# Output weights of a scan layer: rows and means three steps earlier, half of the centring on VectorE

## The chip, the cores and the metric

One core of one Trainium2 chip runs the whole program. The metric is the device time of one execution in microseconds (us), the median of three runs. TensorE (PE) multiplies matrices, VectorE (DVE), ScalarE (ACT) and GpSimd (POOL) work elementwise, SyncE (SP) and POOL issue DMA transfers. Each engine works off its own instructions in order, and the queue of SP as well: a transfer whose inputs are not ready holds all that stand behind it.

## The reference

Two layers on an image batch x of 2 x 768 x 64 x 64 in f32. Cut to what matters, the first layer is:

```
h   = preact(x)                                    # group norm, statistics over the whole image
xs  = conv3x3_depthwise(h @ in_proj_w.T)           # 1536 channels
u   = xs * sigmoid(xs)
dt, B, C = split(u @ x_proj_w.T)                   # 48 + 4 + 4
delta = softplus(dt @ dt_w + dt_b)
s[l]  = exp(delta * A) * s[l-1] + delta * u * B    # scan over 4096 positions, 4 states
y   = sum_n(s * C) + D * u
y   = (y - mean(y)) * rsqrt(var(y) + 1e-5) * ln_g + ln_b   # over the 1536 channels
x1  = x + y @ out_proj_w.T
```

The second layer normalises x1 and is an attention-like product over channels with two 768 x 768 matrices. The edits lie in the first layer, before its scan starts. The kernel folds the normalisation of y into the output weights: with W the 1536 x 768 matrix out_proj_w.T, it needs W scaled by ln_g row by row, less the mean over the 1536 channels of that scaled matrix (a row of 768 numbers, the same for all channels), and as a bias ln_b @ W. "Centring" is that subtraction.

## The kernel before

The image is cut into 16 tiles of 8 rows (512 positions), the 1536 channels into 12 blocks of 128. A chunk is one block of one tile; there are 192 chunks, numbered n for the input projection, a = n - 2 for the convolution, g = n - 17 for the scan. One call of `step(g)` issues the work of all three, so each is a software pipeline written out by hand: the order of instructions on each engine is the order of the calls, and nothing reorders it.

The first sixteen calls (v = 0 to 15, n = v, a = v - 2) only fill the pipeline. In each, PE does `row0(n)` (L348: the first image row for n below 12), `in_proj(n)` (L362) and what `products_of(v)` adds at the end of the step; ACT does `tap_act` (L415, the centre tap into PSUM, `acc`), what `scalar_of(v)` adds, `in_proj_evict` (L374 to L377), `norm_x` (L317, the input of the next tile; three of them at v = 11, needed by `in_proj(12)`), `taps_act` (L427, two taps into buffers) and `silu` (L468). DVE does the remaining taps (`taps_dve`, L461) and the statistics of the second image (L154). POOL adds the two ACT taps by accumulating DMA: `taps_dma` (L439) of chunk a, which waits for the sum of that chunk's taps, and `taps_dma_sum` (L433) of chunk a + 1. SP loads input weights (L323, 384 KB, four buffers), x (L307; one each at v = 6, 7 and 8, three at v = 11, 256 KB each) and the statistics input (L149).

The output weights go along: four loads of three 128 x 768 blocks each (L246, `wg`, at v = 2 to 5), their rows of ln_g @ W and ln_b @ W by PE at v = 11 (`out_weights_rows`, L256, into PSUM tag po0, in three groups of 256 columns), a copy of those rows by ACT (L264), the mean spread over 128 partitions and the bias by PE at v = 12 (L272 and L273, into tag pz), its copy to `wmean` (L277 to L279), twelve scalings by ACT (L283) and twelve subtractions, eight on POOL and four on DVE (L287), in steps 13 to 15, and twelve stores by SP to `wo_dr` in DRAM (L290), from which the out-projection later loads (L329). Blocks 0 to 2 are stored after step 14, the other nine after step 15 and behind it.

Then the pool `l0st` (rows, wmean, pick, wg) is released and the pool `late` takes its place on the same side of SBUF: `ysum`, `bc` (B and C broadcast), `s`, the two `da` buffers of the scan and five tap buffers `tm`. `step(-1)` comes next: `x_dbl` (L491) with its store of B and C to `bc_dr` (L492), the first dt product (`dt_pair`, L502, tag pz) with its softplus, `load_bc` (L495) and the exponentials (L514). `step(0)` begins with the first scan on DVE: L537, L539 and L546.

Of the kernel before, what the change touches and what calls it, by code (L numbers as in the profile page):

```python
# [7 lines left out]
F32 = mybir.dt.float32  # L8
AF = mybir.ActivationFunctionType
ALU = mybir.AluOpType  # L10
# [4 lines left out]
P = 128  # L15
NB, DM, H, W = 2, 768, 64, 64
# [3 lines left out]
NS = 4  # L20
RX = R + 2 * NS
KM = DM // P
# [9 lines left out]
TL = TR * W  # L32
# [8 lines left out]
PC_W, PC_A, PC_D, PC_CB, PC_DB, PC_G, PC_B, PC_N = 0, 9, 13, 14, 15, 16, 17, 18  # L41
# [11 lines left out]
AHEAD = 15  # L53
# [14 lines left out]
def both_layers(  # L68
# [10 lines left out]
    pc = wp.tile([P, KI, PC_N], F32, name="pc")  # L79
# [48 lines left out]
    psZ = ctx.enter_context(tc.tile_pool(name="l0_psz", bufs=1, space=PSUM))  # L128
    psX = ctx.enter_context(tc.tile_pool(name="l0_psx", bufs=1, space=PSUM))
    psO = ctx.enter_context(tc.tile_pool(name="l0_pso", bufs=1, space=PSUM))  # L130
# [114 lines left out]
    def out_weights_load(wg, k):  # L245
        nc.sync.dma_start(wg[k // 3], out_wT[k * P : (k + 3) * P, :].rearrange("(k p) m -> p k m", p=P))  # L246

    MG = 2 * P  # L250

    def out_weights_rows(wg):
        gb = psO.tile([P, 512], F32, tag="po0", name="pgb")
        for k in range(KI):
            for j in range(KM // 2):
                nc.tensor.matmul(  # L256
                    gb[32 * j : 32 * j + 2, :MG], pc[:, k, PC_G : PC_B + 1], wg[k // 3][:, k % 3, j * MG : (j + 1) * MG],
                    start=(k == 0), stop=(k == KI - 1),
                )
        return gb  # L260

    def out_weights_rows_copy(gb, rows):
        for j in range(KM // 2):
            nc.scalar.copy(rows[32 * j : 32 * j + 2, :], gb[32 * j : 32 * j + 2, :MG])  # L264

    def out_weights_mean(rows, pick):
        wm = psZ.tile([P, 2, 512], F32, tag="pz", name="pwm")
        pb = wm[:, 1, MG : MG + KM]
        for j in range(KM // 2):
            for e in range(2):  # L270
                m = 2 * j + e
                nc.tensor.matmul(pb[:, m : m + 1], rows[:, e * P : (e + 1) * P], pick[:, j, P : P + 1], start=True, stop=True)  # L272
            nc.tensor.matmul(wm[:, j // 2, j % 2 * MG : (j % 2 + 1) * MG], pick[:, j, :P], rows, start=True, stop=True)  # L273
        return wm, pb

    def out_weights_mean_copy(wm, pb, wmean):
        nc.scalar.copy(wmean[:, : 2 * MG], wm[:, 0, :])  # L277
        nc.scalar.copy(wmean[:, 2 * MG :], wm[:, 1, :MG])
        nc.scalar.copy(bias_o, pb)  # L279

    def out_weights_scale(wg, k):
        w = wg[k // 3][:, k % 3, :]
        nc.scalar.activation(w, w, AF.Copy, scale=pc[:, k, PC_G : PC_G + 1])  # L283

    def out_weights_sub(wg, wmean, k, engine):
        w = wg[k // 3][:, k % 3, :]
        engine.tensor_sub(w, w, wmean)  # L287

    def out_weights_store(wg, k):
        nc.sync.dma_start(  # L290
            wo_dr[:, k // 3, :, k % 3, :].rearrange("q p m -> p q m"), wg[k // 3][:, k % 3, :].rearrange("p (q m) -> p q m", m=2 * P)
        )
# [50 lines left out]
            )  # L343

    def row0(n):
        p0 = psZ.tile([P, 512], F32, tag="pz", name=f"pa0_{n}")
        for k in range(KM):
            nc.tensor.matmul(p0[:, :W], wis[n][:, k, :], x0s[0][:, k, :], start=(k == 0), stop=(k == KM - 1))  # L348
        nc.scalar.copy(carry[n][:, 1, :], p0[:, :W])
        if n == KI - 1:  # L350
            give(x0s.pop("tile"))
# [803 lines left out]
    with tc.manual_schedule():  # L1155
# [31 lines left out]
        def step(g, prep=None, acts=None):  # L1187
# [13 lines left out]
            if n < KI:  # L1201
                row0(n)
# [148 lines left out]
                norms[g + 2][0][0]()  # L1351

        with tc.tile_pool(name="l0st", bufs=1, side="right") as sp:
            rows = sp.tile([P, MG], F32, name="gb_rows")
            nc.vector.memset(rows, 0.0)
            wmean = sp.tile([P, DM], F32, name="wmean")
            pick = sp.tile([P, KM // 2, P + 1], F32, name="pick")
            nc.sync.dma_start(pick, pick_in)
            wg = [sp.tile([P, 3, DM], F32, name=f"wg{q}") for q in range(KI // 3)]

            first = -AHEAD - 2
            scaled_w = {13: ((0, 1), (2,)), 14: ((3, 4, 5), (6,)), 15: ((7, 8, 9), (10, 11))}
            held = {}

            def products_of(v):
                if v == 11:
                    held["rows"] = out_weights_rows(wg)
                if v == 12:
                    held["mean"] = out_weights_mean(rows, pick)

            def scalar_of(v):
                if v == 12:
                    out_weights_rows_copy(held["rows"], rows)
                if v == 13:
                    out_weights_mean_copy(*held["mean"], wmean)
                for k in sum(scaled_w.get(v, ((), ())), ()):
                    out_weights_scale(wg, k)

            for v in range(AHEAD + 1):
                if 2 <= v < 6:  # L1380
                    out_weights_load(wg, 3 * (v - 2))
                step(first + v, lambda: products_of(v), lambda: scalar_of(v))
                if v == 0:
                    nc.scalar.activation(neg_a, pc[:, :, PC_A : PC_A + NS], AF.Exp)
                    nc.scalar.mul(neg_a, neg_a, -1.0)
                for k in scaled_w.get(v, ((), ()))[0]:
                    out_weights_sub(wg, wmean, k, nc.gpsimd)
                for k in scaled_w.get(v - 1, ((), ()))[1]:
                    out_weights_sub(wg, wmean, k, nc.vector)
                for k in sum(scaled_w.get(v - 1, ((), ())), ()):  # L1390
                    out_weights_store(wg, k)
            for k in scaled_w[AHEAD][1]:
                out_weights_sub(wg, wmean, k, nc.vector)
            for k in sum(scaled_w[AHEAD], ()):
                out_weights_store(wg, k)

        late = right.enter_context(tc.tile_pool(name="l0l", bufs=1, side="right"))

        ysum = late.tile([P, 3, TL], F32, name="ysum")
        bc = late.tile([P, 2 * NS, TL], F32, name="bc")  # L1400
        s = late.tile([P, NS, TL + 1], F32, name="s")

        da1 = late.tile([P, NS, TL + 1], F32, name="da1")
        tm_bufs = [late.tile([P, TL], F32, name=f"tm{j}") for j in (0, 3, 1, 2, 4)]
        tm_bufs = [tm_bufs[j] for j in (0, 2, 3, 1, 4)]
        das = [late.tile([P, NS, TL + 1], F32, name="da0"), da1]
        nc.gpsimd.memset(das[0][:, :, 0], 0.0)
        step(-1)
        nc.gpsimd.memset(das[1][:, :, 0], 0.0)
# [70 lines left out]
@with_exitstack  # L1480
def mamba_then_attention(
    ctx, tc, x, in_wP, xp_wP, dt_wP, out_wT, pc_in, comb_in, pick_in, xsum_in, qkvP, woutP, temp_c, ident_in, gavg_in, gsel_in, hcol_in, hsel_in, esel_in, out
):
    nc = tc.nc
    keep = ctx.enter_context(tc.tile_pool(name="keep", bufs=1))
    dram = ctx.enter_context(tc.tile_pool(name="dram", bufs=1, space=DRAM))
    x1 = [dram.tile([DM, L], F32, name=f"x1_{b}") for b in range(NB)]

    stats1 = [keep.tile([P, KM, 2 * NT + 1], F32, name=f"stats1_{b}") for b in range(NB)]

    ident = keep.tile([P, P], F32, name="ident")
    nc.sync.dma_start(ident, ident_in)
    ones = keep.tile([P, P], F32, name="ones")
    nc.vector.memset(ones, 1.0)
    eps_c = keep.tile([P, 1], F32, name="eps_c")
    nc.vector.memset(eps_c, EPS)
    consts = (ident, ones, eps_c)


    wo_dr = dram.tile([KM // 2, KI // 3, P, 3, 2 * P], F32, name="wo_dr")  # L1500
    bc_dr = [dram.tile([2 * NS, TL], F32, name=f"bc_dr{i}") for i in range(NI)]

    s_dr = {k: dram.tile([KM // 2, 4, P, KM // 2, P], F32, name=f"s_dr_{k}") for k in ("p1", "p3")}
    both_layers(
        tc, nc, consts, x, in_wP, xp_wP, dt_wP, out_wT, pc_in, comb_in, pick_in, xsum_in, gavg_in, gsel_in, wo_dr, bc_dr, s_dr, x1, stats1,
        qkvP, woutP, temp_c, hcol_in, hsel_in, esel_in, [out[b].rearrange("c h w -> c (h w)") for b in range(NB)],
    )
# [105 lines left out]
```

## Time and profile before

| what | us |
|---|---|
| median of three runs | 3709.17 |
| the runs | 3709.97, 3709.17, 3702.92 |
| span of the profiled execution (no other time of that execution is given) | 3708.1 |
| PE, DVE, ACT, POOL busy | 3555.3, 2842.1, 2571.8, 1782.8 |
| first scan operation (L537) starts, from the start of the span | 190.81 |

A line of the timeline reads: start, duration, engine, source line, operation, output <- input, number of instructions, and in brackets how long the engine stood idle before it and what ended that. PE and POOL busy times are as the profile has them; DMA-issuing instructions are on POOL and on SP's queue (SPq). In a line of stretches the columns are the stretch, its sum, then busy time of PE, PE's weight loads, DVE, ACT and POOL, the clock that PE was granted as a share of full, the DMA share and GB/s. Transfers land later than their issue; the landing times are those of their packets in the trace.

### The profile page before, as it was taken

To read this page: it belongs to the slowest core of one execution; us is meant where nothing else is said; L and a number is where in the kernel's file an instruction comes from. 1 tells how busy PE (TensorE), PEld (TensorE's weight loads), DVE (VectorE), ACT (ScalarE), POOL (GpSimd) and SP (SyncE) were. 2 spreads that over 40 slices of the span, in tenths; PEclk is the share of its full clock that TensorE was granted. 3 is DMA by queue.
4 is the path that set the end of the run, shared out by engine and by line. 5 is a ranking of instruction groups with operands and counts; after the bars stand their busy time and mean duration, and the time that the engine had idled before them with its cause. 6 is when DMAs were issued, how large, how long until landed. Compare 5 with 4: busy or idle time off the path is not lost. (4 is left out here: it accounts for less than half of the span.)

```text
span 3708.1 us, 37935 instructions
## 1 busy us (share of the span) xinstructions
PE 3555.3 (96%) x11176; PEld 1771.0 (48%) x11176; DVE 2842.1 (77%) x2571; ACT 2571.8 (69%) x5026; POOL 1782.8 (48%) x1813
## 2 busy tenths in 40 slices
PE   5968999999999999999999999999999999999999
PEld 3423333343333333333344333433347658886688
DVE  7899999999999999999999999997721362224522
ACT  2688889888988898888888988897633542244221
POOL 0355565565655655555556655654443313330232
PEclk9978999999999999999999999999999999999999
DMA  9877888998989899898898989997676538763487
GB/s 354 232 169 162 182 204 185 205 211 191 212 176 209 201 200 208 184 204 185 187 203 194 212 175 211 203 201 177 142 202 183 192 93 265 256 205 123 158 268 245
DMA packets 380301, 738.98 MB, mean 199 GB/s; under 512 B 44304, under 2 KB 116944, under 8 KB 376000
## 3 DMA queue, kind: packets, MB, share of 16 engines
q0 software_dynamic: 146208, 270.08, 42.6%
q1 hardware_dynamic: 233888, 466.49, 38.4%
q8 instruction: 90, 1.47, 0.2%
q14 instruction: 115, 0.94, 0.1%
HBM read 440.96 MB, written 60.03 MB: 135 GB/s over the span
## 5 line engine op out<-in xcount | busy, mean ns | idle before, releaser
L362 PE MATMUL pa<-u,w 128*128 128x512 f32 (+1 forms) x2304 | 1035.8, 599 | 7.5 <-ACT carry L377 7.3
L603 PE MATMUL po<-u,w 128*128 128x512 f32 x2256 | 1011.5, 598 | 8.1 <-DVE u L615 7.9
L539 DVE TENSOR_TENSOR_SCAN s<-da,s 128x2052 f32<-128x2052 f32 x192 | 851.1, 4433 | 19.5 <-DVE s L537 0.9
L362 PEld LDWEIGHTS pa<-u,w 128*128 128x128 f32 x2304 | 429.5, 192 | 597.7 <-issue 484.7
L603 PEld LDWEIGHTS po<-u,w 128*128 128x128 f32 x2256 | 420.8, 190 | 582.7 <-issue 551.3
L526 POOL TENSOR_TENSOR ysum<-da 128x1024 f32<-128x1024 f32 x192 | 386.8, 2015 | 547.4 <-DVE da L546 464.1
L461 DVE SCALAR_TENSOR_TENSOR acc<-xs,pc,acc 128x512 f32<-128x512 f32 x698 | 525.6, 753 | 29.2 <-ACT acc L415 12.7
L537 DVE TENSOR_TENSOR s<-du,bc 128x2048 f32<-128x2048 f32 x192 | 439.2, 2288 | 83.0 <-POOL du L518 73.8
L433 POOL DMA_DIRECT2D tm<-tm x309 | 270.3, 875 | 462.7 <-ACT tm L427 423.5
L514 ACT ACTIVATE da<-dl,neg_a 128x512 f32<-128x512 f32 x768 | 489.6, 713 | 0.0
L546 DVE TENSOR_TENSOR da<-s,bc 128x2048 f32<-128x2048 f32 x192 | 440.0, 2292 | 6.3
L533 POOL DMA_DIRECT2D u<-ysum x384 | 380.4, 1255 | 4.2 <-issue 3.5
L427 ACT ACTIVATE tm<-xs,pc 128x512 f32<-128x512 f32 x486 | 317.1, 717 | 15.1 <-DMA tm<-tm 7.3
L415 ACT ACTIVATE acc<-xs,pc 128x512 f32<-128x512 f32 x192 | 132.2, 688 | 215.7 <-DVE u L461 206.4
L518 POOL TENSOR_TENSOR du<-dl,u 128x512 f32<-128x512 f32 x192 | 246.5, 1284 | 0.0
L439 POOL DMA_DIRECT2D u<-tm x177 | 206.1, 1164 | 59.6 <-issue 50.1
L447 PE MATMUL acc<-xs,dg 128*128 128x512 f32 x264 | 140.0, 641 | 50.0 <-ACT acc L415 49.6
L886 PE MATMUL po_p<-v,w 128*128 128x256 f32 x672 | 171.9, 380 | 1.4 <-ACT po_p L983 1.4
L886 PE MATMUL po_p<-u,w 128*128 128x256 f32 x624 | 159.7, 379 | 0.0
L461 DVE SCALAR_TENSOR_TENSOR u<-xs,pc,acc 128x512 f32<-128x512 f32 x192 | 143.6, 748 | 7.7
L831 POOL TENSOR_TENSOR v<-u 128x256 f32<-128x256 f32 x21 | 15.7, 758 | 277.1 <-ACT u L849 262.1
L886 PE MATMUL acc_p<-u,w 128*128 128x256 f32 x556 | 143.7, 382 | 4.6 <-DMA w<-woutP 3.4
(285 smaller groups left out, 5006.5 us busy)
## 6 DMA issues: line engine op xcount, KB each, us to landing
u<-ysum POOLq DMA_DIRECT2D x384, 256.0 KB, 5.5
tm<-tm POOLq DMA_DIRECT2D x309, 256.0 KB, 4.3
w<-in_wP SPq DMA_DIRECT2D x192, 384.0 KB, 4.4
w<-wo_dr SPq DMA_DIRECT2D x192, 384.0 KB, 4.7
u<-x SPq DMA_DIRECT2D x263, 256.0 KB, 4.8
w<-s_dr_p SPq DMA_DIRECT2D x288, 192.0 KB, 3.4
u<-tm POOLq DMA_DIRECT2D x177, 256.0 KB, 5.8
bc<-bc_dr SPq DMA_DIRECT2D x32, 1024.0 KB, 7.7
```

The source lines that it names most:

```text
L362: nc.tensor.matmul(pa[:, :nn], w[:, k, :], xts[i, k][:, :nn], start=(k == 0), stop=(k == KM - 1))
L427: nc.scalar.activation(tm.rearrange("p (h w) -> p h w", w=W), xs[:, dy : dy + TR, dx : dx + W], AF.Copy, scale=pc[:, c, PC_W + j : PC_W + ...
L433: nc.gpsimd.dma_start(tms[a][0], tms[a][q], accum_op=ALU.add)
L461: nc.vector.scalar_tensor_tensor(dst, xs[:, dy : dy + TR, dx : dx + W], pc[:, c, PC_W + j : PC_W + j + 1], acc, ALU.mult, ALU.add)
L514: nc.scalar.activation(das[g % 2][:, n, 1:], deltas[g], AF.Exp, scale=neg_a[:, c, n : n + 1])
L526: nc.gpsimd.tensor_add(ysum[:, 0 : 2 + g % 2 : 1 + g % 2, :], da[:, 0:2, 1:], da[:, 2:4, 1:])
L533: nc.gpsimd.dma_start(us[g], ysums(g, n), accum_op=ALU.add)
L537: nc.vector.tensor_mul(s[:, :, 1:], dus.pop(g).unsqueeze(1).to_broadcast([P, NS, TL]), bc[:, :NS, :])
L539: nc.vector.tensor_tensor_scan(sf, das[g % 2].rearrange("p n l -> p (n l)"), sf, 0.0, ALU.mult, ALU.add)
L546: nc.vector.tensor_mul(das[g % 2][:, :, 1:], s[:, :, 1:], bc[:, NS:, :])
L603: nc.tensor.matmul(po[e], w[:, kk, e * P : (e + 1) * P], us[i * KI + k], start=(k == 0), stop=(k == KI - 1))
L886: nc.tensor.matmul(dst, half[:, k, :], tiles[blocks[seq[i][0]][:3]][what][k], start=(start and k == 0), stop=(k == KH - 1), skip_group_che ...
```

## The change

It does five things. The rows are computed at v = 8 and the mean at v = 9. The rows are formed in four column groups of 192, not three of 256, and the mean by four products of 192 columns with twelve short ones of 64 for the bias. Scales, centring and stores are spread over v = 9 to 15: blocks 0, 2, 4, 6 and 9 are scaled by ACT a step before POOL subtracts the mean (v = 10 to 14), and blocks 1, 3, 5, 7, 8, 10 and 11 are scaled and centred by one DVE scalar_tensor_tensor that reads the mean from PSUM (v = 11 to 15); each step's blocks are stored right after that step. PSUM tags change hands: the rows take pz, `row0` takes po0, the mean stays in pz until the last centring. And the buffers of `late` are allocated in another order, `da0` and three of the `tm` first.

```diff
--- before.py
+++ after.py
@@ -247,44 +247,51 @@
 
 
 
-    MG = 2 * P
+    MJ = DM // 4
+    HP = P // 2
 
     def out_weights_rows(wg):
-        gb = psO.tile([P, 512], F32, tag="po0", name="pgb")
+        gb = psZ.tile([P, 2, 512], F32, tag="pz", name="pgb")[:, 0, :]
         for k in range(KI):
-            for j in range(KM // 2):
+            for j in range(4):
                 nc.tensor.matmul(
-                    gb[32 * j : 32 * j + 2, :MG], pc[:, k, PC_G : PC_B + 1], wg[k // 3][:, k % 3, j * MG : (j + 1) * MG],
+                    gb[32 * j : 32 * j + 2, :MJ], pc[:, k, PC_G : PC_B + 1], wg[k // 3][:, k % 3, j * MJ : (j + 1) * MJ],
                     start=(k == 0), stop=(k == KI - 1),
                 )
         return gb
 
     def out_weights_rows_copy(gb, rows):
-        for j in range(KM // 2):
-            nc.scalar.copy(rows[32 * j : 32 * j + 2, :], gb[32 * j : 32 * j + 2, :MG])
+        for j in range(4):
+            nc.scalar.copy(rows[32 * j : 32 * j + 2, :], gb[32 * j : 32 * j + 2, :MJ])
 
     def out_weights_mean(rows, pick):
         wm = psZ.tile([P, 2, 512], F32, tag="pz", name="pwm")
-        pb = wm[:, 1, MG : MG + KM]
-        for j in range(KM // 2):
-            for e in range(2):
-                m = 2 * j + e
-                nc.tensor.matmul(pb[:, m : m + 1], rows[:, e * P : (e + 1) * P], pick[:, j, P : P + 1], start=True, stop=True)
-            nc.tensor.matmul(wm[:, j // 2, j % 2 * MG : (j % 2 + 1) * MG], pick[:, j, :P], rows, start=True, stop=True)
+        pb = wm[:, 1, 2 * MJ : 2 * MJ + KM]
+        for h in range(2 * KM):
+            m, e = divmod(h, 2)
+            j, o = divmod(h * HP, MJ)
+            nc.tensor.matmul(
+                pb[e * HP : (e + 1) * HP, m : m + 1], rows[:, o : o + HP], pick[:, j, P : P + 1], start=True, stop=True
+            )
+        for j in range(4):
+            nc.tensor.matmul(wm[:, j // 2, j % 2 * MJ : (j % 2 + 1) * MJ], pick[:, j, :P], rows, start=True, stop=True)
         return wm, pb
 
     def out_weights_mean_copy(wm, pb, wmean):
-        nc.scalar.copy(wmean[:, : 2 * MG], wm[:, 0, :])
-        nc.scalar.copy(wmean[:, 2 * MG :], wm[:, 1, :MG])
+        nc.scalar.copy(wmean, wm[:, :, : 2 * MJ])
         nc.scalar.copy(bias_o, pb)
 
     def out_weights_scale(wg, k):
         w = wg[k // 3][:, k % 3, :]
         nc.scalar.activation(w, w, AF.Copy, scale=pc[:, k, PC_G : PC_G + 1])
 
-    def out_weights_sub(wg, wmean, k, engine):
-        w = wg[k // 3][:, k % 3, :]
-        engine.tensor_sub(w, w, wmean)
+    def out_weights_sub(wg, wmean, k):
+        w = wg[k // 3][:, k % 3, :].rearrange("p (h m) -> p h m", h=2)
+        nc.gpsimd.tensor_sub(w, w, wmean)
+
+    def out_weights_centre(wg, wm, k):
+        w = wg[k // 3][:, k % 3, :].rearrange("p (h m) -> p h m", h=2)
+        nc.vector.scalar_tensor_tensor(w, w, pc[:, k, PC_G : PC_G + 1], wm[:, :, : 2 * MJ], ALU.mult, ALU.subtract)
 
     def out_weights_store(wg, k):
         nc.sync.dma_start(
@@ -343,7 +350,7 @@
             )
 
     def row0(n):
-        p0 = psZ.tile([P, 512], F32, tag="pz", name=f"pa0_{n}")
+        p0 = psO.tile([P, 512], F32, tag="po0", name=f"pa0_{n}")
         for k in range(KM):
             nc.tensor.matmul(p0[:, :W], wis[n][:, k, :], x0s[0][:, k, :], start=(k == 0), stop=(k == KM - 1))
         nc.scalar.copy(carry[n][:, 1, :], p0[:, :W])
@@ -1351,29 +1358,31 @@
                 norms[g + 2][0][0]()
 
         with tc.tile_pool(name="l0st", bufs=1, side="right") as sp:
-            rows = sp.tile([P, MG], F32, name="gb_rows")
+            rows = sp.tile([P, MJ], F32, name="gb_rows")
             nc.vector.memset(rows, 0.0)
-            wmean = sp.tile([P, DM], F32, name="wmean")
-            pick = sp.tile([P, KM // 2, P + 1], F32, name="pick")
+            wmean = sp.tile([P, 2, DM // 2], F32, name="wmean")
+            pick = sp.tile([P, 4, P + 1], F32, name="pick")
             nc.sync.dma_start(pick, pick_in)
             wg = [sp.tile([P, 3, DM], F32, name=f"wg{q}") for q in range(KI // 3)]
 
             first = -AHEAD - 2
-            scaled_w = {13: ((0, 1), (2,)), 14: ((3, 4, 5), (6,)), 15: ((7, 8, 9), (10, 11))}
+            centred = {
+                10: ((0,), ()), 11: ((2,), (1,)), 12: ((4,), (3,)), 13: ((6,), (5,)), 14: ((9,), (7, 8)), 15: ((), (10, 11))
+            }
             held = {}
 
             def products_of(v):
-                if v == 11:
+                if v == 8:
                     held["rows"] = out_weights_rows(wg)
-                if v == 12:
+                if v == 9:
                     held["mean"] = out_weights_mean(rows, pick)
 
             def scalar_of(v):
-                if v == 12:
+                if v == 9:
                     out_weights_rows_copy(held["rows"], rows)
-                if v == 13:
+                if v == 10:
                     out_weights_mean_copy(*held["mean"], wmean)
-                for k in sum(scaled_w.get(v, ((), ())), ()):
+                for k in centred.get(v + 1, ((), ()))[0]:
                     out_weights_scale(wg, k)
 
             for v in range(AHEAD + 1):
@@ -1383,27 +1392,23 @@
                 if v == 0:
                     nc.scalar.activation(neg_a, pc[:, :, PC_A : PC_A + NS], AF.Exp)
                     nc.scalar.mul(neg_a, neg_a, -1.0)
-                for k in scaled_w.get(v, ((), ()))[0]:
-                    out_weights_sub(wg, wmean, k, nc.gpsimd)
-                for k in scaled_w.get(v - 1, ((), ()))[1]:
-                    out_weights_sub(wg, wmean, k, nc.vector)
-                for k in sum(scaled_w.get(v - 1, ((), ())), ()):
+                on_pool, on_vector = centred.get(v, ((), ()))
+                for k in on_pool:
+                    out_weights_sub(wg, wmean, k)
+                for k in on_vector:
+                    out_weights_centre(wg, held["mean"][0], k)
+                for k in on_pool + on_vector:
                     out_weights_store(wg, k)
-            for k in scaled_w[AHEAD][1]:
-                out_weights_sub(wg, wmean, k, nc.vector)
-            for k in sum(scaled_w[AHEAD], ()):
-                out_weights_store(wg, k)
 
         late = right.enter_context(tc.tile_pool(name="l0l", bufs=1, side="right"))
 
+        da0 = late.tile([P, NS, TL + 1], F32, name="da0")
+        tm_bufs = {j: late.tile([P, TL], F32, name=f"tm{j}") for j in (1, 2, 4)}
         ysum = late.tile([P, 3, TL], F32, name="ysum")
+        tm_bufs.update({j: late.tile([P, TL], F32, name=f"tm{j}") for j in (0, 3)})
         bc = late.tile([P, 2 * NS, TL], F32, name="bc")
         s = late.tile([P, NS, TL + 1], F32, name="s")
-
-        da1 = late.tile([P, NS, TL + 1], F32, name="da1")
-        tm_bufs = [late.tile([P, TL], F32, name=f"tm{j}") for j in (0, 3, 1, 2, 4)]
-        tm_bufs = [tm_bufs[j] for j in (0, 2, 3, 1, 4)]
-        das = [late.tile([P, NS, TL + 1], F32, name="da0"), da1]
+        das = [da0, late.tile([P, NS, TL + 1], F32, name="da1")]
         nc.gpsimd.memset(das[0][:, :, 0], 0.0)
         step(-1)
         nc.gpsimd.memset(das[1][:, :, 0], 0.0)
@@ -1544,8 +1549,8 @@
     comb[[0, 32], 0, :] = 1.0 / DI
     comb[[64, 96], 1, :] = 1.0 / DI
 
-    pick = np.zeros((P, KM // 2, P + 1), np.float32)
-    for j in range(KM // 2):
+    pick = np.zeros((P, 4, P + 1), np.float32)
+    for j in range(4):
         pick[32 * j, j, :P] = 1.0 / DI
         pick[32 * j + 1, j, P] = 1.0
```

## The prediction

> **What bounds the kernel now.** I read the page first (PE busy 96% of the span, so the layers themselves are PE's), then the 40 slices, whose first one is the only one with PE under 0.8 (5968...). The edits all lie in that start, the sixteen fill steps before the first scan, so I went to the waits between 110 and 200 us:
>
> ```profile
> DVE s L537 <- DMA bc<-bc_dr: 8.3, 1, 8.3
> POOL da L1407 <- DMA wo_dr<-wg: 5.9, 1, 5.9
> ACT tm L427 <- DMA wo_dr<-wg: 5.4, 1, 5.4
> ```
>
> The first scan waits for the broadcast of B and C; the two others wait for the stores of the output weights. The timeline of SP, POOL, DVE and PE (start, duration, engine, line) shows how these meet:
>
> ```profile
> 119.46 1.37 SPq L307 DMA_DIRECT2D u<-x  x3
> ...
> 157.17 2.68 SPq L290 DMA_DIRECT2D wo_dr<-wg  x3
> ...
> 169.79 9.98 SPq L290 DMA_DIRECT2D wo_dr<-wg  x9
> ...
> 183.53 0.81 SPq L495 DMA_DIRECT2D bc<-bc_dr  x2
> ```
> ```profile
> 141.49 0.89 POOL L433 DMA_DIRECT2D u<-u  x1
> ...
> 164.51 5.66 POOL L287 TENSOR_TENSOR wg<-wg,wmean 128x768 f32<-128x768 f32 x3
> ...
> 172.28 5.65 POOL L287 TENSOR_TENSOR wg<-wg,wmean 128x768 f32<-128x768 f32 x3
> ```
> ```profile
> 164.09 8.64 DVE L287 TENSOR_TENSOR wg<-wg,wmean 128x768 f32<-128x768 f32 x3
> ...
> 190.81 2.29 DVE L537 TENSOR_TENSOR s<-du,bc 128x2048 f32<-128x2048 f32 x1 [8.25 <-DMA bc<-bc_dr]
> ```
>
> Read backwards: POOL's last subtraction ends at 177.9, SP issues the last store at 179.13, it lands at 183.48 (4.35 us), and at 183.53 the broadcast starts. Its first half lands at 190.32 and the scan begins 0.49 us later. The broadcast waits for all twelve stores although its buffer reaches over the first group of weights only, by the order of allocation, and that group had landed at 164.78: the wait is for the whole pool. After 190.81 DVE runs some dozen steps without a wait and PE follows, so a shift of the first scan carries to the end one to one. The number to predict is when that scan starts.
>
> **The change, part by part.** *Rows and means three steps sooner.* The PE rows they cost now are:
>
> ```profile
> 133.55 5.36 PE L256 MATMUL pgb<-wg,pc 128*2 128x256 f32 x72
> 138.84 5.42 PE L362 MATMUL pa<-u,w 128*128 128x512 f32 x12
> ```
>
> 72 passes in 5.29 us are 73.5 ns a pass. Four groups make 96 passes of 192 columns. If the pace follows columns and groups (73.5 x 3/4 x 3/4 = 41 ns) that is 4.0 us, if it follows passes 7.1; no row decides it, I take the middle, 5.6. The mean took 2.64 us (144.09 to 146.73). Now it has 24 short passes, between 92 ns (L272's four in 0.37) and half of that, since each loads 64 columns of weights where L272's loads 128, and 8 of 192 columns at 0.19 (L273's two of 256 in 0.51, by columns): 2.6 to 3.7, taken 3.3. So PE carries 8.9 us (6.6 to 10.8) two to four steps sooner; in_proj(10) ends near 135.9 instead of 126.97 and in_proj(11) near 142.4. By itself this costs nothing later, since the same work leaves steps 11 and 12.
>
> A rule speaks against the four groups: the Trainium skill, "TensorE: Matmul & The Clock Gate", section "Wait — 56ns, not 53.3ns?", has the sequencer spend about 62 ns on each MATMUL where hardware decode is off. By it 96 passes take 6.0 us as an estimate, more than the 5.29 measured for 72; no row here shows such a floor for this shape.
>
> *Stores sooner, and what they stand in front of.* Each store now follows its step. In the order of the changed build, SP's queue after step 10 is store 0, the weights of in_proj(13), one statistics load, then the three x loads of tile 1 that in_proj(12) needs. Store 0 waits for POOL's subtraction 0, which stands behind L433 of a=9. That L433 was issued at 141.49 (its ACT input would now be ready near 139 to 141, so nothing brings it sooner). Add its 0.89 and one subtraction (3.91 for two, 2.0): 144.4. Then four SP issues of some 0.42 to 0.46: the x loads go out at 145.6 to 146.5 where they went at 119.46 to 120.41. They landed 5.2 to 6.6 us after issue; the last now lands near 152.4.
>
> Queued behind: ACT's three L317 are in order ahead of the tap copies of a=10, so ACT holds from about 146 to 150.8. in_proj(12) starts near 142.4, finds k=3 to 5 missing, and ends near 154.2 (last norm 153.2, one us of passes): in_proj(13), 146.73 before, is 7.5 us later. The tap copies end at 154.5, ACT's acc(11) at 155.9 (1.33, 0.71, 0.68 after the norm; 138.95 before).
>
> The second hold is the same: L433 of a=10 at 154.5, subtraction 2 until 157.4, stores 2 and 1, and only then, at 158.2, the weights of in_proj(14) and the statistics load. Behind three transfers of 384 KB at about 1 us each, at the page's median of 4.4 us, the weights land near 163; in_proj(14) would be ready at 161.4 and waits 1.6. The statistics input lands near 164.
>
> *Centring on DVE.* Seven operations from PSUM replace four subtractions (0.94 each, one 6.9) and, on ACT, seven of twelve scales (0.82 to 0.93). No row shows a 768-element scalar_tensor_tensor; L461's 512 take 0.75, in columns 1.13, and the subtraction's 0.94 is the other end; I take 1.1. DVE's own sum from a=11: taps from 155.9, 6.2 us (138.98 to 145.19), end 162.1; then the statistics wait to 164; two of them 1.2; centre 5 1.1; taps of a=12 4.6; statistics 0.6; centres 7 and 8 2.2; taps of a=13 4.6; statistics 1.3; centres 10 and 11 2.2: the last ends at 181.8. POOL, with five subtractions where eight were, is no longer late: subtraction 9 ends near 176. ACT's x_dbl copy loses the scales in front of it (164.63 4.24) but comes near 177.5 because PE is late, not 168.76.
>
> *What is late next.* Store 11 goes out at 181.8 and lands 3.4 (L290's median) to 4.35 us later: 185.2 to 186.2. The broadcast takes 6.8 again (183.53 to 190.32), the scan starts 0.49 later: 192.5 to 193.5, against 190.81. So 1.7 to 2.7 late. Two covers are thin. The means stay in PSUM until centre 11, so the first dt product, 169.39 before, waits to 181.8 and goes ahead of in_proj(16): softplus, two tables (1.28 each) and four exponentials (2.54) end near 191. DVE's taps of a=14 and a=15 (4.6 each and 0.6) end near 191.7. Were the broadcast early, the scan would begin near 192 anyway.
>
> *Column groups in the copies, PSUM tags of row0:* one copy of 768 for two, 0.1 us on an ACT that waits later anyway. Row0's new tag costs nothing, since po0 is otherwise used by no one until the out-projection; 0.2 if its copy were late (L349 took 0.21). *Scan buffers reordered:* in the built order POOL's memset, ACT's first tm and the broadcast still wait for all twelve stores; zero, at most 1.3 us off if it worked (from 193.5 to the 192 of DVE's own sum).
>
> *PE clock.* The granted clock fell after PE's short gaps:
>
> ```profile
> 175.00:180.00 5.00, 2.63 (x6) 0.86 (x5) 4.84 (x7) 1.97 (x5) 2.93 (x2) 0.91 1.10 339
> 180.00:185.00 5.00, 5.00 (x10) 1.96 (x8) 2.44 (x4) 1.37 (x3) 0.73 (x2) 0.75 0.95 308
> ```
>
> Five us at 0.75 lose 1.25; the hold of in_proj(12) can bring such a stretch at 154, and the second another: 0 to 2.5, mostly off DVE's path; I add 0.6. The same skill page, section "What's actually happening", gives half clock after an idle window of about 3.4 us; a hold of 8 us meets that, and the estimate by it is 1.7 us lost in the window after it; in this trace gaps of 2.06 and 2.37 us went with the 0.91 and 0.75 above already.
>
> Sum: 2.2 and 0.6, near +3. The profiled execution spans 3708.1, 1.1 us below the median 3709.17; the shift is put on the median: 3712.
>
> **Rivals.** *Slower: the loads behind the stores land late.* Of the u<-x loads between 117 and 200 us the median landing was 9.7, not 5.2 to 6.6, under DMA shares about 1. If the three x loads take 9.7 and the weights of in_proj(14) lose as much again (about 3.3 each), DVE's sum moves by 7 and the clock by 1.5 more: +11, 3720. It decides once the x loads take more than 8 us. For it: stores, accumulating DMAs and loads now come together near 146 and 158; against: the DMA share from 140 to 170 was 0.68.
>
> *Faster: the holds do not bite.* If subtraction 0 runs before L317 needs its inputs, or PE's waiting is taken up elsewhere, then x_dbl comes near 168, the last store at 169, it lands at 172.4, the broadcast at 179.2 to 179.7, and DVE's taps of a=15, no longer behind the 6.9 us subtraction, end at 179.7: the scan at 180, -10.8, 3698. It needs the x loads to land by 142, so subtraction 0 done by 135; L433 of a=9 at 141.49 speaks against it. For it speaks what the waits show: 17.4 us of SP behind POOL's subtractions, 8.3 of DVE behind the broadcast.
>
> *The reorder frees the buffers after all:* +1.5, 3711, inside the forecast's range; the pool-wide wait of the broadcast at 183.53 speaks against it.
>
> **How the numbers follow.** Forecast (holds of about 7.5 and 1.6, stores end near 182): 0.50, own range 3707 to 3717 from -1 (all low ends: four-group pace 4.0, landing 3.4, no clock loss, and the runs' spread) to +7. Slower: 0.30. Faster: 0.20. The range takes in most of both: 3699 to 3722. 0.2% is 7.4 us, about what a measurement of this kernel can tell from no change (the three runs spread over 7.05). Slower by more: 0.29 of the slower case and 0.06 of the forecast's upper end, 0.35; faster by more: 0.19; the rest 0.46.
>
> **What would show it.** Right: L307's last x3 in the fill at 145 to 147, L317 waiting for them some 4 us or more, in_proj(13) near 154, the last centre near 182, last store landing near 186, the scan near 193, and the wait for bc_dr shortened to about 1. Wrong: x loads before 140, or no wait of ACT there; the last store landed before 176 (the faster case); a centre of several us; memset or tm starting before the last landing.

## The result and the profile after

The changed kernel takes 3713.34 us, the median of 21 runs (3707.99 to 3720.15), against 3707.95 for the kernel before in the same measurement. The ratio is 1.0015, with an interval of 1.0009 to 1.0021: slower by some 5 us, inside the forecast (3712, 3699 to 3722) and under the 0.2% that the forecast called no difference. More runs than the three of before resolve it. The first scan, the mark that the prediction followed, starts at 195.40 us instead of 190.81, 4.6 later. The one profiled execution of the changed kernel spans 3708.3 (its time was 3710.21, 3.1 under the median of the 21) and does not show the loss in its span: the scans of chunks 1 to 10 are still 4.6 to 5.0 later than in the profile of before, that of chunk 140 is 0.3 sooner and the last one 0.6 later. One pair of profiles tells the place of a shift, not its sum.

The source lines moved by seven: L317 is now L324, L307 is L314, L433 and L439 are L440 and L446, L537 is L544; the subtraction on POOL is L290, the centring on DVE L294, the store L297. First the waits between 110 and 205 us (engine, line, what it waited for: us in all, times, longest):

```profile
ACT u L324 <- DMA u<-x: 8.5, 2, 8.3
POOL da L1412 <- DMA wo_dr<-wg: 8.3, 1, 8.3
PE pa L369 <- ACT u L324: 7.3, 1, 7.3
PE pz L509 <- DVE wg L294: 4.8, 1, 4.8
DVE s L544 <- POOL du L525: 3.6, 1, 3.6
```

The first and the third are new: before, ACT had no such wait for x in these steps, and PE none for ACT's norms. The second was 5.9. The fourth stands where PE had waited 2.1 us for ACT's copy of the dt inputs, the fifth where before had DVE's 8.3 us for the broadcast. The longest waits of SP's queue for POOL, the timeline of that queue, POOL's first subtraction and ACT's wait show the cause of the first:

```profile
SPq L297 <- POOL wg L290: 41.4, 5, 20.7
```
```profile
142.09 0.38 SPq L297 DMA_DIRECT2D wo_dr<-wg  x1
...
143.59 1.40 SPq L314 DMA_DIRECT2D u<-x  x3
...
180.62 1.78 SPq L297 DMA_DIRECT2D wo_dr<-wg  x2
...
189.69 0.81 SPq L502 DMA_DIRECT2D bc<-bc_dr  x2
```
```profile
139.25 0.88 POOL L440 DMA_DIRECT2D u<-u  x1
139.89 2.17 POOL L290 TENSOR_TENSOR wg<-wg,wmean 128x768 f32<-128x768 f32 x1
```
```profile
149.91 0.81 ACT L324 ACTIVATE u<-u,xbias,xscale 128x512 f32<-128x512 f32 x1 [8.27 <-DMA u<-x]
```

SP waited up to 20.7 us for POOL's subtraction, and the three x loads, which had gone out at 119.46, left at 143.59, behind store 0, a weight load and a statistics load. They landed at 149.89, 150.92 and 151.66. PE in the same stretch:

```profile
112.75 4.08 PE L257 MATMUL pgb<-wg,pc 128*2 128x192 f32 x96
...
123.44 0.87 PE L273 MATMUL pwm<-pick,gb_rows 128*64 128x1 f32 x24
124.24 1.57 PE L277 MATMUL pwm<-gb_rows,pick 128*128 128x192 f32 x8
...
150.78 10.85 PE L369 MATMUL pa<-u,w 128*128 128x512 f32 x18 [7.35 <-ACT u L324]
...
181.66 2.08 PE L509 MATMUL pz<-xd,dt_w 48*128 48x512 f32 x4 [4.75 <-DVE wg L294]
183.67 7.19 PE L369 MATMUL pa<-u,w 128*128 128x512 f32 x12
```

The rows and the mean come early and cheap. in_proj(12) stops half way for 7.35 us, and the rest of it and in_proj(13), 18 passes, take 10.8 us where before's spacing of 0.437 (5.24 for twelve) makes 7.9. The dt product waits for the last centring, and in_proj(16) behind it takes 7.19 instead of 5.42. In both places the granted clock (the last column but two, a mean over the stretch) was down:

```profile
150.00:165.00 15.00, 14.22 (x30) 5.76 (x31) 6.43 (x9) 12.07 (x22) 6.48 (x6) 0.78 0.69 193
...
180.00:185.00 5.00, 3.34 (x6) 1.35 (x7) 4.86 (x7) 3.00 (x4) 0.86 (x1) 0.54 0.96 262
```

The trace's own record of the granted clock has it at one half from 146.31 to 156.55 and from 180.44 to 187.27, and at full between. PE worked 5.77 and 5.61 us of these two stretches.

Last, the end of the story on DVE, and on ACT and POOL:

```profile
164.61 1.29 DVE L154 BATCH_NORM_STATS2 st_in<-xg 128x6 f32<-128x512 f32 x2 [3.38 <-DMA xg<-x]
...
179.59 1.92 DVE L294 SCALAR_TENSOR_TENSOR wg<-wg,pc,pwm 128x768 f32<-128x768 f32 x2
...
195.40 2.29 DVE L544 TENSOR_TENSOR s<-du,bc 128x2048 f32<-128x2048 f32 x1 [3.62 <-POOL du L525]
```
```profile
190.90 0.59 ACT L382 COPY xs<-pa 128x512 f32<-128x512 f32 x1 [3.63 <-PE pa L369]
...
191.54 1.34 ACT L434 ACTIVATE tm<-xs,pc 128x512 f32<-128x512 f32 x2
```
```profile
193.17 0.86 POOL L440 DMA_DIRECT2D tm<-tm  x1 [1.79 <-ACT tm L434]
...
193.77 1.60 POOL L525 TENSOR_TENSOR du<-dl,u 128x512 f32<-128x512 f32 x1
```

Between DVE's first and second line it has no wait at all: from the late statistics load on, its own work sets the last centring, and with it the last store. The first scan then waits for `du` (delta times u, formed by POOL), which ends at 195.37: POOL issues the sum of the last tap copies first, and those copies follow ACT's eviction of in_proj(16). The first half of the broadcast had landed at 194.17.

### The profile page after: what moved, and what is told of

Its sections match the earlier page's. It is cut to its first block, busy times and chain, and to the rows that moved or that the text cites. A ratio compares the mean times of both kernels' runs of the same rounds, so it can differ in the third digit from the quotient of the medians.

```text
span 3708.3 us, 37997 instructions
## 1 busy us (share of the span) xinstructions
PE 3552.1 (96%) x11214; PEld 1770.8 (48%) x11214; DVE 2839.6 (77%) x2574; ACT 2565.6 (69%) x5019; POOL 1775.0 (48%) x1810
## 5 line engine op out<-in xcount | busy, mean ns | idle before, releaser
L544 DVE TENSOR_TENSOR s<-du,bc 128x2048 f32<-128x2048 f32 x192 | 439.2, 2287 | 77.8 <-POOL du L525 77.6
L440 POOL DMA_DIRECT2D tm<-tm x309 | 270.4, 875 | 461.2 <-ACT tm L434 387.5
L446 POOL DMA_DIRECT2D u<-tm x177 | 205.2, 1159 | 51.8 <-issue 36.0
```

The lines of the kernel that those rows point to most:

```text
L440: nc.gpsimd.dma_start(tms[a][0], tms[a][q], accum_op=ALU.add)
L544: nc.vector.tensor_mul(s[:, :, 1:], dus.pop(g).unsqueeze(1).to_broadcast([P, NS, TL]), bc[:, :NS, :])
```

## The experiments

Theory A is the forecast's: the stores make SP hold loads that the projections need, and this costs more than the earlier centring gains. Rival B puts the loss on the mean that stays in PSUM until the last centring. Rival C is the order of the buffers. The start of the first scan, read from one profile of each version, shows smaller differences than the time does; both are given. All ratios are to the kernel before, measured again with each set (medians 3708.14 with the first four versions, 3707.59 with the others).

**Stores behind the next step's loads.** One edit to the changed kernel:

```diff
-                for k in on_pool + on_vector:
+                for k in pending:
                     out_weights_store(wg, k)
+                pending = on_pool + on_vector
+            for k in pending:
+                out_weights_store(wg, k)
```

> The changed kernel with each step's stores issued after the SP loads of the next step (the last ones still after step 15); nothing else moves. Theory A, loads held behind stores that wait for POOL: the x loads of tile 1 go out near 120 again, in_proj(12) has no wait of ACT's norms (7.35 us in the changed kernel), the first scan starts near 182 (195.40 changed, 190.81 before), time near 3700, 13 below the changed kernel and 7 below before. Rival B, the loss comes from the mean that stays in PSUM until the last centring (dt product late, clock down): the holds were taken up anyway, the scan still starts at 193 to 195 and the time stays within 2 of 3713.

Its time is 3702.66 (ratio 0.9989, 0.9979 to 0.9998) and its scan starts at 183.12. From the timelines of SP, PE and DVE:

```profile
123.89 1.87 SPq L314 DMA_DIRECT2D u<-x  x3
```
```profile
134.95 15.67 PE L369 MATMUL pa<-u,w 128*128 128x512 f32 x36
...
170.94 7.63 PE L369 MATMUL pa<-u,w 128*128 128x512 f32 x12
```
```profile
183.12 2.29 DVE L544 TENSOR_TENSOR s<-du,bc 128x2048 f32<-128x2048 f32 x1 [4.06 <-DMA bc<-bc_dr]
```

The x loads go out twenty us sooner and three projections run as one group of 36 passes without a gap. The mean still stays in PSUM until the last centring: PE waits 3.03 us for it and in_proj(16) takes 7.63, so what rival B names is still there, and the scan is 12.3 sooner than in the changed kernel. (The line names the broadcast as DVE's releaser; it landed at 181.62, and du, which ended at 183.09, came later.) A is right and B, as the main cause, is out. This version beats the kernel before as well, by some 5 us.

**Only the three x loads sooner.** In the fill, k = 3 to 5 are loaded at step 10, not 11, so ahead of store 0:

```diff
-                    for k in {6: [0], 7: [1], 8: [2], 11: [3, 4, 5]}.get(c, []):
+                    for k in ({6: [0], 7: [1], 8: [2], 10: [3, 4, 5]} if i == 0 else {6: [0], 7: [1], 8: [2], 11: [3, 4, 5]}).get(c, []):
                         load_x(i + 1, k)
```

> The changed kernel with the three x loads of tile 1 (k = 3 to 5) issued one step sooner, so that they stand ahead of store 0 in SP's queue; the weights of in_proj(13) and (14) and the statistics still stand behind stores. Theory A says that these three loads are most of it: ACT's norms no longer wait, the tap copies of a = 10 come near 142 and with them POOL's subtraction 2, so the second hold shrinks too; scan near 185, time near 3703. If the hold of the weights matters by itself, scan 188 to 192. Rival B: 193 to 195, time near 3713.

3706.49 (0.9997, 0.9988 to 1.0006), scan at 189.47. Its PE and DVE:

```profile
149.75 8.32 PE L369 MATMUL pa<-u,w 128*128 128x512 f32 x12 [4.15 <-DMA w<-in_wP]
```
```profile
189.47 2.29 DVE L544 TENSOR_TENSOR s<-du,bc 128x2048 f32<-128x2048 f32 x1 [3.39 <-DMA bc<-bc_dr]
```

This is the middle one of the three expectations. With the x loads out of the way in_proj(13) waits 4.15 us for its weights, which stand behind the same store 0, and then runs at lower clock (8.32). DVE waits up to 7.5 us for a statistics load behind it. So of the 12.3 us the x loads alone are worth 5.9, and what else stands behind the stores 6.4: moving one transfer out of the queue uncovers the next. The time alone does not tell this version from the kernel before.

**The buffers in the old order.** The changed kernel with `ysum`, `bc`, `s`, `da1`, the `tm` and `da0` allocated as before.

> The changed kernel with the scan buffers allocated in the order of before. Theory A: the order frees nothing, since first uses wait for all twelve stores: scan at 195.4 give or take 0.5, time 3713 within 2. Rival C, the addresses matter: a difference of more than 4 us either way.

3713.86 (1.0012, 1.0003 to 1.0021), and POOL's memset still waits 8.4 us for the stores:

```profile
195.77 2.29 DVE L544 TENSOR_TENSOR s<-du,bc 128x2048 f32<-128x2048 f32 x1 [3.80 <-POOL du L525]
```

The scan starts 0.4 from where it does in the changed kernel. Rival C is out: the order makes no difference here.

**The steps of before, the centring of the changed kernel.**

```diff
-                10: ((0,), ()), 11: ((2,), (1,)), 12: ((4,), (3,)), 13: ((6,), (5,)), 14: ((9,), (7, 8)), 15: ((), (10, 11))
+                13: ((0,), (1, 2)), 14: ((3, 4), (5, 6)), 15: ((7, 8), (9, 10, 11))
...
-                if v == 8:
+                if v == 11:
                     held["rows"] = out_weights_rows(wg)
...
```

The mean follows at step 12, and scales, DVE's part and stores stand in the steps where they stood before.

> Rows, mean, scales, subtractions and stores in the steps of before (11, 12, 13 to 15), but with the four column groups, seven of twelve blocks centred by DVE from PSUM, the tags and the buffers of the changed kernel. Theory A: without stores ahead of loads the DVE centring is a gain: POOL has five subtractions and not eight, DVE no operation of 6.9 us; the last store goes out near 175 instead of 179, the scan starts near 187, time near 3704. Rival B: the mean in PSUM until the last centring holds the dt product (169.39 before) and the scan starts at 191 or later, time 3708 or more.

3706.18 (0.9999, 0.9989 to 1.0009), scan at 189.11:

```profile
166.71 4.70 DVE L294 SCALAR_TENSOR_TENSOR wg<-wg,pc,pwm 128x768 f32<-128x768 f32 x5
...
189.11 2.29 DVE L544 TENSOR_TENSOR s<-du,bc 128x2048 f32<-128x2048 f32 x1 [7.88 <-DMA bc<-bc_dr]
```

Five centrings take 4.70 us where three subtractions took 8.64. But nine stores still went out in one burst, the last of them at 177.84, 1.3 sooner and not 4: POOL's last two subtractions (4.22 us from 171.45) still stood late, and SP took its stores in order behind them. The scan gained 1.7, not the 4 expected, and lies between the two expectations, as the time does, which cannot be told from before. A's size was off here; the scan's sign was A's. The dt product waits 3.9 us for the mean, and the scan is still no later than before.

**The first buffers in their own pool.** `da0` and three of the `tm` are allocated from a pool opened before the weights' pool, so that they take none of the weights' place.

```diff
+        early = right.enter_context(tc.tile_pool(name="l0e", bufs=1, side="right"))
+        da0 = early.tile([P, NS, TL + 1], F32, name="da0")
+        tm_bufs = {j: early.tile([P, TL], F32, name=f"tm{j}") for j in (1, 2, 4)}
         with tc.tile_pool(name="l0st", bufs=1, side="right") as sp:
...
-        da0 = late.tile([P, NS, TL + 1], F32, name="da0")
-        tm_bufs = {j: late.tile([P, TL], F32, name=f"tm{j}") for j in (1, 2, 4)}
```

> The changed kernel with the first da buffer and three tap buffers in a pool of their own that does not take the weights' place, so that their first uses no longer wait for the stores (8.3 us of POOL at the memset in the changed kernel). Theory D, the last link is PE: the dt product waits 4.75 us for the last centring, in_proj(16) runs at half clock and ACT's tap copies come after its eviction at 190.9 anyway: scan still at 195 give or take 0.7. Rival E, the wait for the stores is the last link: scan near 194.2 less 0 to 1, where the broadcast landed, that is 193.5 to 194.6.

One run: 3704.72, which by itself can't be placed. From POOL and DVE:

```profile
181.06 0.44 POOL L1413 MEMSET da<- 128x4 f32 x1
```
```profile
194.92 2.29 DVE L544 TENSOR_TENSOR s<-du,bc 128x2048 f32<-128x2048 f32 x1 [3.40 <-DMA bc<-bc_dr]
```

The scan was ended by the broadcast (landed 194.60). POOL's memset runs at 181.06 without the 8.3 us wait, yet du still ends at 194.5, since the sum of the taps before it waits for ACT's taps of a = 15, and those for in_proj(16) at low clock (evicted at 190.0). The scan lies in theory D's band and just outside the rival's, but the broadcast was 0.1 us later than du here: the two links are as good as tied, and the run does not tell them apart.

**The last two means from SBUF.**

```diff
-                    out_weights_centre(wg, held["mean"][0], k)
+                    out_weights_centre(wg, held["mean"][0] if k < 10 else wmean, k)
```

> The changed kernel with the last two centrings (blocks 10 and 11) reading the mean from its copy in SBUF, so that PSUM tag pz is free some 8 us sooner. Theory D: the dt product goes out near 177.6 instead of 181.66 and in_proj(16) near 179 instead of 183.67; the taps then wait for the stores at 189.6 and the broadcast (194.17) is last: scan at 194.2 to 194.8, 0.6 to 1.2 sooner. Rival E: no change, 195.4.

One run: 3713.65, scan at 195.47. Its PE and DVE:

```profile
176.69 1.13 PE L509 MATMUL pz<-xd,dt_w 48*128 48x512 f32 x4 [0.68 <-ACT xd L498]
```
```profile
195.47 2.29 DVE L544 TENSOR_TENSOR s<-du,bc 128x2048 f32<-128x2048 f32 x1 [3.83 <-DMA bc<-bc_dr]
```

The dt product goes out 5 us sooner and du ends at 193.55, as expected, but the broadcast lands at 195.15, a us later than in the changed kernel, and takes over. The number came out as the rival's, the intermediate steps as theory D's; why the broadcast took a us longer stays open. Both links, PE to du and store to broadcast, end within 0.1 to 1.6 us of each other in these three versions; taking away either leaves the other.

**Both fixes, and the first half of the broadcast ahead of the stores.** The later stores with the means from SBUF:

> Stores one step later (as in the experiment of that name, scan at 183.12) and the last two centrings from SBUF. The dt product goes out near 166.2 instead of 168.94, ACT's eviction of in_proj(16) near 174 instead of 178.61, exponentials end near 180 instead of 183; the broadcast, issued at 175.6, stays last: scan at 182.5 to 183, time 3702 within 3.

3703.98 (0.9992, 0.9983 to 1.0001):

```profile
182.70 2.29 DVE L544 TENSOR_TENSOR s<-du,bc 128x2048 f32<-128x2048 f32 x1 [4.62 <-POOL du L525]
```

The scan and the time are as expected, the scan 0.4 sooner than without the second fix. The last link is not the expected one: in_proj(16) runs at full pace again (5.42), ACT's part has slack (the exponentials end at 179.4) and the broadcast lands at 181.51, but du, in POOL's queue behind two accumulating transfers, ends at 182.67. Then, on top, the buffer of B apart and outside the weights' place:

```diff
-        nc.sync.dma_start(bc[:, h * NS : (h + 1) * NS, :], bc_dr[i][h * NS : (h + 1) * NS, :].partition_broadcast(P))
+        nc.sync.dma_start(bcs[h], bc_dr[i][h * NS : (h + 1) * NS, :].partition_broadcast(P))
...
+        early = right.enter_context(tc.tile_pool(name="l0e", bufs=1, side="right"))
+        bc_b = early.tile([P, NS, TL], F32, name="bc_b")
+        tm_bufs = {j: early.tile([P, TL], F32, name=f"tm{j}") for j in (1, 2, 4)}
...
```

> As the run before, and the half of the broadcast buffer that the scan reads first (B), with three tap buffers, lies in a pool of its own that does not take the weights' place; C, s and both da wait for the stores as ever. If the pool-wide wait is what holds the broadcast, its first half goes out near 171.5 instead of 175.6 and lands near 178; da's first use stays at 175.7, so the exponentials end near 179.5: scan at 179.5 to 180.5, time near 3699.5. If the traffic of the stores themselves sets the landing, the scan stays at 182 to 183.

3701.97 (0.9983, 0.9974 to 0.9992), scan at 188.15. The broadcast goes out at 172.40, 3.2 sooner, and lands at 182.17, 0.7 later. Its packets begin at 176.69, after the last packet of the five stores (176.24); in the version before they began at 177.26. So the issue came 3.2 us sooner, the first packet 0.6: the broadcast still stood behind the same stores. The accumulating transfer of a = 14, whose packets now end at 183.86 beside the broadcast's, lands 12.1 us after its issue, where it took 7.9, and POOL holds du behind it:

```profile
185.03 0.86 POOL L446 DMA_DIRECT2D u<-u  x1 [7.98 <-DMA u<-u]
```
```profile
188.15 2.29 DVE L544 TENSOR_TENSOR s<-du,bc_b 128x2048 f32<-128x2048 f32 x1 [8.52 <-POOL du L525]
```

Both expectations missed the scan. The condition of the second, that the stores themselves set the landing, fits the packets. That the broadcast's traffic slowed the accumulating transfer fits these times, but no run tests it. That the median is no worse than that of the kernel whose scan starts 5 us sooner is not explained by this; the intervals of this version, of the one before it and of the first experiment overlap, and which of the three is best stays open.

## Why the prediction was right, step by step

The sign and the first part of the mechanism held: store 0 behind POOL's subtraction, the x loads at 143.59 (forecast 145.6), the norms, the pause of in_proj(12), the late statistics input (forecast near 164, DVE's line begins at 164.61), DVE's chain of taps and centrings without a gap, the last one ending at 181.5 (forecast 181.8). By scan starts against 190.81 the parts are: centring with groups, steps as before, -1.7; three steps sooner without the holds, a further -6.0 (189.11 to 183.12); the holds, +12.3. The sum is +4.6.

The last part did not hold. The forecast let the scan wait about 1 us for the broadcast and start near 193; it waited 3.62 us for du and started at 195.40. The size came out near because errors offset each other: the stores landed later, the broadcast was quicker, and a link that the forecast had not added up ended last. That much of the agreement is luck.

What was off, term by term:

- *PE's price.* The rows took 4.0 us, the low end of 4.0 to 7.1, which is the pace by columns and groups (42 ns a pass against 73.5). The mean took 2.3, below its range of 2.6 to 3.7: the 24 short passes took 0.80 us, 33 ns each. The estimate of 6.0 us for the rows, from the rule of about 62 ns a MATMUL with hardware decode off (the Trainium skill, "TensorE: Matmul & The Clock Gate", section "Wait — 56ns, not 53.3ns?"), does not fit this trace, in which the passes of one set of four start 6 to 7 ns apart; the measurement decides. The waits before the scan show none of it.
- *The first hold.* It came 2 us sooner: the accumulating transfer ahead of subtraction 0 went out at 139.25, where the forecast left it at 141.49 and held that nothing would bring it sooner. The x loads then took 6.3 to 7.1 us to land, not 5.2 to 6.6, and ACT waited 8.27.
- *The clock.* Taken at 0.6 us. The 18 passes after the pause alone lost 2.9, the dt product 0.95 and in_proj(16) some 1.8, after a wait of 4.75 us. The forecast read the 0.91 and 0.75 of the kernel before as the effects of two gaps, of 2.06 and 2.37 us. The clock record has one drop there, to one half from 179.06 to 182.47, after the second gap, and full clock after the first. The rule of the same page (section "What's actually happening"), half clock after an idle window of about 3.4 us, agrees in the size of the step, and the waits of 7.35 and 4.75 us meet it; but 2.37 us sufficed in the kernel before, and the measurement decides. The forecast held the loss to be mostly off the path. In in_proj(16) it was on it, through the tap copies that wait for that projection's eviction (190.90 against 177.43 before), to du, with the broadcast 1.2 us behind.
- *The second hold.* Forecast 1.6 us for in_proj(14); it did not wait for its weights at all. They landed at 162.46, but in_proj(13), delayed by the pause and the lower clock, ended at 161.55, and the products of L482 kept PE busy until 163.42.
- *The last stores.* They landed 8.1 us after the last issue, near 189.6, not 3.4 to 4.35. The packets of the last two begin at 184.22, after those of a weight load issued ahead of them (183.85), with accumulating transfers beside them. This was the largest mis-sized term, 3.7 to 4.7 more; the broadcast behind them took 4.5, not 6.8, and gave 2.3 back.
- *The covers.* Named as thin, they were: du at 195.37 passed the broadcast at 194.17. The forecast's cover, near 191, names softplus, tables and exponentials on ACT. It does not name the eviction of in_proj(16) and the tap copies, which stand ahead of the exponentials in ACT's order (these end at 195.3), nor du, which POOL forms behind an accumulating transfer of those copies. The lower clock in the dt product and in_proj(16) makes some 2.7 us of the difference; the rest is what was not named.
- *One to one.* The forecast let a shift of the first scan carry to the end. Against the kernel before, the times moved by +5.4 (changed), -5.5, -1.7, +5.7 and -2.0 us (the first four experiments) where the scans moved by +4.6, -7.7, -1.3, +5.0 and -1.7: right in sign and within 2.2 us of each other. For the last two versions it does not come out: -3.6 for -8.1 and -5.6 for -2.7.

Of the rivals, the faster one was tested by removing its obstacle: without the holds the scan starts at 183.1, not 180, with the broadcast still behind five stores and du behind POOL's accumulating transfers. The slower one, late landings, did happen at the stores and not at the x loads.

## What to carry to other kernels

When a store is issued sooner, ask what waits for its data and what stands behind it in the same queue: a store that is not ready holds every load after it. Here, issued behind the loads of the next step, the same stores turned a loss of 5 us into a gain of 5. Moving one held transfer only uncovered the next, so move the one that holds. And when several chains end within a microsecond or so of each other, expect the removal of any single one to show nothing.

## What the runs showed of the hardware that was not expected

Products with weights of 2 columns ran side by side in column groups: in the kernel before, three passes of 256 columns start 7 ns apart and the next three 215 ns after the first; in the changed kernel, four passes of 192 columns start 6 to 7 ns apart and the next four 162 ns after the first. That is 42 ns a pass against 73.5, and 4.0 us for the same columns that took 5.3. Products of one column with 64-column weights came in pairs, 58 ns from pair to pair (0.80 us for 24). PE lost half its clock for 3.4 us after a wait of only 2.37 us. A broadcast of 1 MB issued 3.2 us sooner, but still behind five stores of 384 KB, landed 0.7 us later, and an accumulating transfer beside it took 4.2 us longer. And one centring that ran beside POOL's subtraction took 1.00 us (DVE 165.81, POOL 164.54 to 166.66), where before one subtraction with both inputs from SBUF had taken 6.9 beside POOL's.
